# A transformer block with channel attention: the attention's norms read from PSUM, its PSUM copies on another engine, and a new order of the work

## The chip, the cores and the metric

The kernel runs on one core of a Trainium2 chip. The core has five engines with instruction queues of their own: TensorE (PE, matrix products; its weight loads are shown apart as PEld), VectorE (DVE), ScalarE (ACT), GpSimd (POOL) and SyncE (SP, which here only starts transfers). Each engine works through its queue in the order in which the program was written. The metric is the device time in microseconds from the first to the last instruction; the median of several executions counts.

## The reference, cut to what matters

The input is 16 images of 128 channels and 96 x 96 pixels in float32. Two residual steps follow each other:

```
xn1  = layernorm over channels(x)
q, k, v = xn1 @ wq.T, xn1 @ wk.T, xn1 @ wv.T        # 8 heads of 16 channels, over 9216 pixels
q, k = q / |q|, k / |k|                             # norms over the pixels, one for each channel
attn = softmax((q k^T) / 4)                         # 16 x 16 for each head
x    = x + (attn v) @ wp.T

xn2  = layernorm over channels(x)
h    = w_in xn2                                     # 1x1, to 512 channels
h    = depthwise 3x3 (h), then gelu
x    = x + w_out h                                  # 1x1, back to 128 channels
```

Since the attention works over channels and not over pixels, everything it needs of an image is the Gram matrix G = z z^T (128 x 128) of the normalized pixels z and their sum s. With the layer norm's scale folded into the weights and its shift b in bias terms c = W b, the inner product of two projected channels is w_i G w_j + (w_i s) c_j + c_i (w_j s) + N c_i c_j, with N = 9216 pixels. The squared norm of channel i is the same with i = j: w_i G w_i + 2 c_i (w_i s) + N c_i c_i.

## The kernel before, in words

**Tiling.** An image is cut into 8 bands of 12 rows (`BR`), a band into 3 units of 4 rows (`UR`, 384 pixels). Channels lie on the 128 partitions. The 512 hidden channels are four chunks of 128.

**Stages for an image.** `norm(i, False)` transposes pixels (`forth`, L572), takes the statistics (`stats`, L579, VectorE), computes the reciprocal deviation on GpSimd (L586, L590), scales on ScalarE (`scaled`, L617), adds the pixels into the Gram bank `g` in PSUM (`gram`, L631) and transposes back (`back`, L662; `place`, L668). `attention(s, i)` (L700 to L820) turns G and s into a 128 x 128 matrix `mwT` and a column `d`. `norm(i, True)` applies them (`mix`, L530; `mixed`, L539), adds x, and normalizes again (L572, L579, L621, L662, L666). Then `conv_job` makes one chunk of one band: 1x1 products on TensorE (`hidden`, L845), their copies from PSUM to SBUF on ScalarE (`kept`, L850), the nine taps of the depthwise filter partly as products on ScalarE (L861) that are added by accumulating transfers (L869), partly on VectorE (`tap`, L865, 128 x 1152 elements each), then gelu on ScalarE (L873). In some bands the fourth chunk is computed on TensorE instead (`by_matmuls`, L916, gelu L922). `ffn_out` makes the output product (L939) and adds it to x on VectorE (L946).

**Attention before.** It is a chain of 16 steps, each on one engine, in one PSUM bank. VectorE copies G and s from PSUM (`gs`, L728). TensorE transposes s to a row (L733), which VectorE copies (`srow`, L737). TensorE computes u = G W (L742), adds the one-partition bias term s c to it (L743), and makes the row s W (L745). VectorE copies u (L752), makes the row sW + N c (L753), and then the elementwise products u * W (L755) and (sW + N c) * c (L756), all 256 columns wide for q and k together and kept in a large tile `wide` that is taken from the pool of x tiles. TensorE sums both down the partitions for the norms (L763, L764) and makes k q^T from u and the rows (L769, L770). VectorE bounds the norms (L774), GpSimd takes the power -1/2 (L778), VectorE scales (L782, L784), TensorE transposes (L788), ScalarE takes the exponential (L793), VectorE masks, sums and divides (L798 to L801), TensorE makes the product with the output projection (L805), VectorE copies it (`y`, L809), TensorE makes the last two products (L813, L814) and VectorE copies them out (`mwT`, `d`, L818, L819).

**What sets the order.** Every piece of work is handed to a planner (`Plan.op`) with its engine, an assumed duration in ns, the tokens it reads and writes, and a due place. The due place is a number of conv jobs plus an offset for the kind of work from the table `AT`; at the same engine the smaller one goes first. `Plan.order` plays the program with the assumed durations, buffers and queues, and the work is then written out in the order of the starts that came out. This is done while the program is built; on the chip each engine keeps that order and waits where it must. So a change to an assumed duration, to a token or to the table moves instructions anywhere in the program. Image 0's attention uses one of four PSUM banks `h` that the other products share; the later images' use the Gram bank `g` itself, of which there is only one. `wide` stands on one of the two tiles of the x pool (`x1`).

Of the kernel before, what the change touches and what calls it, by code (L numbers as in the profile page):

```python
# [9 lines left out]
F32 = mybir.dt.float32  # L10
AF = mybir.ActivationFunctionType
ALU = mybir.AluOpType
# [6 lines left out]
BR = 12  # L19
# [10 lines left out]
X1_BUFS, XB_BUFS, PR_BUFS, H3_BUFS, ZT_BUFS = 2, 6, 5, 10, 3  # L30
IN_TURN = ("tr", "h3", "pr", "xb", "x1")
AT = dict(
    weights=5.95, zeros=1.3, load_a=-24.9, forth_a=-15.4, stats_a=-14.45, variance_a=-16.5, power_a=0.1,
    scaled_a=-8.2, gram=-10.45, back_a=-24.05, place_a=-20.25, attention=-20, mix=-9.75, residual=-0.2,
    mixed=-5.2, add_x=13.3, forth_b=-13.25, stats_b=-9.65, variance_b=-14, power_b=-10.85, shift_b=-26,
    scaled_b=4.45, back_b=-25.35, place_b=4.85, halo=7.55, hidden=0.1, kept=-2.95, product=-12.5,
    products=4.8, add_last=-15, tap=3.1, add_first=31.85, gelu=-8.35, conv=-0.05, conv_gelu=-13.5,
    out=4.05, add=-3.25, store=7.05,
)
STEP = dict(scaled=0.3, hidden=0.1, products=0.5, tap=0.166, conv=1.6, conv_tap=0.03, out=0.8, out_part=0.05)  # L40
SLACK = 300
# [164 lines left out]
def tile_restormer_block(  # L206
# [24 lines left out]
    nc = tc.nc  # L231
    B, C, H, W = x.shape
    P = 128
# [6 lines left out]
    NTOK = H * W  # L240
# [20 lines left out]
    ident = const.tile([P, P], F32, name="ident")  # L261
# [3 lines left out]
    ones = const.tile([P, 1], F32, name="ones")  # L265
# [15 lines left out]
    nc.scalar.dma_start(out=dw, in_=w_dw.rearrange("(n p) o kh kw -> p n (o kh kw)", p=P))  # L281

    wvb = const.tile([P, 1], F32, name="wvb")
    none = const.tile([P, 1], F32, name="none")
    wqkT = const.tile([P, 2 * P], F32, name="wqkT")
    cqk = const.tile([1, 2 * P], F32, name="cqk")
# [10 lines left out]
    keep = ctx.enter_context(tc.tile_pool(name="keep", bufs=2))  # L297
# [37 lines left out]
    grams, mats, h3s, staged = {}, {}, {}, {}  # L335
# [3 lines left out]
    op = plan.op  # L339
# [59 lines left out]
    def weights(p):  # L399

        mine = [("h3", ("weights", k)) for k in range(2)]
        v, names = staged, iter(range(99))
# [36 lines left out]
        def centred():  # L439
            pc = v["pc2"] = bank(("weights", "centred"))  # L440
            nc.tensor.matmul(pc[:, : 2 * P], lhsT=v["centre"], rhs=wqkT, start=True, stop=True)
            nc.tensor.matmul(pc[:, 2 * P : 3 * P], lhsT=v["wvT"], rhs=v["w1centre"], start=True, stop=True)
            nc.tensor.matmul(pc[:, 3 * P : 3 * P + 1], lhsT=v["wvT"], rhs=b1, start=True, stop=True)

        def keep_centred():
            nc.vector.tensor_copy(wqkT, v["pc2"][:, : 2 * P])
            nc.vector.tensor_copy(wv_sb, v["pc2"][:, 2 * P : 3 * P])
            nc.vector.tensor_copy(wvb, v["pc2"][:, 3 * P : 3 * P + 1])

        def biases():  # L450
            v["pc"] = bank(("weights", "biases"))[:1, : 2 * P]
# [23 lines left out]
        pc = ("h", ("weights", "centred"))  # L475
# [224 lines left out]
    def attention(s, i):  # L700


        places_of = dict(srow="ma", kq="ma", em="ma", y="ma", gs="mb", e="mb", a="mb")
        columns = dict(ps_s=128, ps_u=256, ps_r=0, ps_n=128, ps_kq=256, ps_qk=384, ps_y=0, ps_m=128, ps_d=256)
        v = {}
        apart = i == 0
        mine = [("h", ("attention", i)) if apart else ("g", i), ("m", i)]

        def sb(shape, tag, pool=att):
            v[tag] = pool.tile(shape, F32, tag=places_of.get(tag, tag), name=f"{tag}_{i}")  # L710
            return v[tag]

        def ps(shape, tag):

            c = columns[tag]
            v[tag] = (bank(("attention", i)) if apart else grams[i])[: shape[0], c : c + shape[1]]
            return v[tag]

        def step(engine, ns, also=()):
            def add(f):  # L720
                op(engine, ns, s, f, [("w", "qk")], [*mine, *also], ns + 200 + SLACK)
            return add

        wide = [("x1", ("attention", i))]

        @step("DVE", 210, [("g", i)])
        def _():
            nc.vector.tensor_copy(sb([P, P + 1], "gs"), grams[i][:, : P + 1])  # L728
            v["gsb"], v["s"] = v["gs"][:, :P], v["gs"][:, P:]

        @step("PE", 220)
        def _():
            nc.tensor.matmul(ps([1, P], "ps_s"), lhsT=v["s"], rhs=ident, start=True, stop=True)  # L733

        @step("DVE", 200)
        def _():
            nc.vector.tensor_copy(sb([1, P], "srow"), v["ps_s"])  # L737

        @step("PE", 1290)
        def _():  # L740

            nc.tensor.matmul(ps([P, 2 * P], "ps_u"), lhsT=v["gsb"], rhs=wqkT, start=True, stop=False)  # L742
            nc.tensor.matmul(v["ps_u"], lhsT=v["srow"], rhs=cqk, start=False, stop=True)  # L743

            nc.tensor.matmul(ps([1, 2 * P], "ps_r"), lhsT=v["s"], rhs=wqkT, start=True, stop=True)  # L745

        @step("DVE", 1400, wide)
        def _():
            t = x1pool.tile([P, BR * W], F32, tag="x", name=f"wide_{i}")
            for k, (rows_, tag) in enumerate([(P, "u"), (1, "srqk"), (P, "prod"), (1, "prow")]):  # L750
                v[tag] = t[:rows_, 2 * P * k : 2 * P * (k + 1)]
            nc.vector.tensor_copy(v["u"], v["ps_u"])  # L752
            nc.vector.scalar_tensor_tensor(v["srqk"], cqk, float(NTOK), v["ps_r"], ALU.mult, ALU.add)  # L753

            nc.vector.tensor_mul(v["prod"], v["u"], wqkT)  # L755
            nc.vector.tensor_mul(v["prow"], v["srqk"], cqk)  # L756

        @step("PE", 1320, wide)
        def _():
            pn = ps([P, 2], "ps_n")  # L760
# [11 lines left out]
        @step("DVE", 80)  # L772
# [12 lines left out]

        @step("PE", 110)
        def _():
            nc.tensor.transpose(ps([P, P], "ps_qk"), v["kq"], ident)  # L788

        @step("ACT", 2900)  # L790
        def _():

            nc.scalar.activation(sb([P, P], "e"), v["ps_qk"], AF.Exp, scale=v["rq"])  # L793

        @step("DVE", 700)
        def _():
# [10 lines left out]
        @step("DVE", 200)  # L807
        def _():
            nc.vector.tensor_copy(sb([P, P], "y"), v["ps_y"])  # L809

        @step("PE", 300)
        def _():
            nc.tensor.matmul(ps([P, P], "ps_m"), lhsT=wv_sb, rhs=v["y"], start=True, stop=True)  # L813
            nc.tensor.matmul(ps([P, 1], "ps_d"), lhsT=v["y"], rhs=wvb, start=True, stop=True)  # L814

        @step("DVE", 290)
        def _():
            nc.vector.tensor_copy(sb([P, P], "mwT", keep), v["ps_m"])  # L818
            nc.vector.tensor_copy(sb([P, 1], "d", keep), v["ps_d"])  # L819
            mats[i] = v["mwT"], v["d"]  # L820

    def h3_of(g, n):
# [201 lines left out]
```

## Time and profile before

| | before |
|---|---|
| time, median of 3 | 4276.48 us (4270.45 to 4277.21) |
| profiled span | 4280.8 us |
| VectorE taps, L865 | 3554.6 us busy in 2592 instructions |
| ScalarE products, L861 | 1907.7 us busy in 1422 instructions (1307.9 and 599.8) |
| TensorE conv, output and hidden products, L916, L939, L845 | 1305.4, 1158.5 and 1043.3 us busy |
| first tap starts | 98.64 us |
| attention of image 1, first to last copy | 224.57 to 251.30 us |

The page gives busy time of each engine, the span in 40 slices, the chain of work that ended last, and the costliest groups of instructions. In a group's line stand the source line, the engine, the operation, the output and inputs by name, shapes, count, and behind the bar the busy time, the mean duration and the idle time of the engine ahead of the group with what ended it. Durations of neighbours on one engine overlap a little, so that the sum of durations is larger than the time they hold the engine. A line of the timeline has the start, the length, engine, line, operation and, in brackets, idle time and what ended it. A line of the waits has the waiting engine and line, the one waited for, the total, the number and the longest.

### The profile page before, as it was taken

To read this page: it belongs to the slowest core of one execution; us is meant where nothing else is said; L and a number is where in the kernel's file an instruction comes from. 1 tells how busy PE (TensorE), PEld (TensorE's weight loads), DVE (VectorE), ACT (ScalarE), POOL (GpSimd) and SP (SyncE) were. 2 spreads that over 40 slices of the span, in tenths; PEclk is the share of its full clock that TensorE was granted. 3 is DMA by queue.
4 is the path that set the end of the run, shared out by engine and by line. 5 is a ranking of instruction groups with operands and counts; after the bars stand their busy time and mean duration, and the time that the engine had idled before them with its cause. 6 is when DMAs were issued, how large, how long until landed. Compare 5 with 4: busy or idle time off the path is not lost.

```text
span 4280.8 us, 52546 instructions
## 1 busy us (share of the span) xinstructions
PE 4201.1 (98%) x17453; PEld 2677.0 (63%) x17453; DVE 4141.5 (97%) x4766; ACT 4074.4 (95%) x7278; POOL 2423.4 (57%) x2331
## 2 busy tenths in 40 slices
PE   8999999999999999999999999999999999999999
PEld 6566666666666666666666665666656666666555
DVE  6999999999999999999999999999999999999999
ACT  4999999999999999999999999999999999999996
POOL 4556556555556556656565665556656555555432
PEclk9999999999999999999999999999999999999999
DMA  2889899998998989989898998989889898998997
GB/s 86 181 181 202 184 200 196 191 199 187 194 195 191 193 186 209 194 186 204 178 194 185 192 200 179 198 186 202 184 181 201 187 198 190 191 194 168 187 187 162
DMA packets 197887, 802.87 MB, mean 188 GB/s; under 512 B 22896, under 2 KB 24304, under 8 KB 197616
## 3 DMA queue, kind: packets, MB, share of 16 engines
q0 software_dynamic: 158112, 647.70, 78.3%
q1 hardware_dynamic: 37152, 151.01, 9.7%
q8 instruction: 138, 2.26, 0.2%
q10 hardware_dynamic: 2352, 0.81, 0.1%
q14 instruction: 133, 1.09, 0.1%
HBM read 148.26 MB, written 75.50 MB: 52 GB/s over the span
## 4 chain that ended last, share of the span: by engine, by line
PE 55%; ACT 21%; DVE 14%; DMA 5%; issue 3%; POOL 2%; ACTq 0%; POOLq 0%; DVEq 0%
PE h L916 16%; PE h L939 13%; DVE h L865 12%; PE h L845 11%; ACT pr L861 5%; DMA h<-pr 3%; PE g L631 3%; PE h L530 3%; ACT h L850 3%; ACT h L861 2%; ACT zT L621 2%; ACT h L873 2%; PE pB_a L662 2%; PE pB_b L662 2%; ACT zT L617 2%
## 5 line engine op out<-in xcount | busy, mean ns | idle before, releaser
L865 DVE SCALAR_TENSOR_TENSOR h<-h,dw,h 128x1152 f32<-128x1152 f32 x2592 | 3554.6, 1409 | 17.3 <-ACT h L861 14.0
L861 ACT ACTIVATE pr<-h,dw 128x1152 f32<-128x1152 f32 x976 | 1307.9, 1357 | 9.7 <-DMA pr<-pr 9.4
L916 PE MATMUL h<-xn,comp 128*128 128x384 f32 x3564 | 1305.4, 487 | 5.0 <-ACT h L850 3.1
L939 PE MATMUL h<-h,woutT 128*128 128x384 f32 x3072 | 1158.5, 489 | 7.3 <-ACT h L850 3.4
L845 PE MATMUL h<-xn,winT 128*128 128x384 f32 (+1 forms) x2676 | 1043.3, 501 | 5.4 <-ACT h L850 2.7
L916 PEld LDWEIGHTS h<-xn,comp 128*128 128x128 f32 x3564 | 652.4, 190 | 420.6 <-ACT h L850 13.5
L869 POOL DMA_DIRECT2D pr<-pr x531 | 498.8, 939 | 680.8 <-ACT pr L861 478.2
L939 PEld LDWEIGHTS h<-h,woutT 128*128 128x128 f32 x3072 | 560.1, 190 | 356.6 <-issue 15.0
L850 ACT COPY h<-h 128x384 f32<-128x384 f32 (+1 forms) x1338 | 702.0, 590 | 34.1 <-PE h L845 25.0
L869 POOL DMA_DIRECT2D h<-pr x445 | 437.9, 993 | 503.5 <-DVE h L865 117.3
L845 PEld LDWEIGHTS h<-xn,winT 128*128 128x128 f32 x2676 | 484.4, 190 | 323.7 <-issue 53.1
L861 ACT ACTIVATE h<-h,dw 128x1152 f32<-128x1152 f32 x446 | 599.8, 1347 | 5.1 <-PE h L939 3.2
L873 ACT ACTIVATE h<-h 128x1152 f32<-128x1152 f32 x448 | 556.6, 1243 | 42.2 <-DMA h<-pr 39.9
L590 POOL TENSOR_TENSOR rstd_a<-ve_a,mhalf 128x4 f32<-128x4 f32 x288 | 520.0, 1806 | 11.4 <-POOL ve_a L586 0.2
L590 POOL TENSOR_TENSOR rstd_b<-ve_b,mhalf 128x4 f32<-128x4 f32 x288 | 492.8, 1715 | 10.3
L621 ACT ACTIVATE zT<-pT_b,nb_b,rstd_b 128x128 f32<-128x128 f32 x1132 | 452.4, 559 | 6.4 <-DVE nb_b L594 6.4
L586 POOL TENSOR_SCALAR ve_b<-st_b 128x4 f32<-128x4 f32 x288 | 286.4, 994 | 260.0 <-DVE st_b L579 254.2
L586 POOL TENSOR_SCALAR ve_a<-st_a 128x4 f32<-128x4 f32 x288 | 292.6, 1016 | 227.1 <-DVE st_a L579 223.0
L617 ACT ACTIVATE zT<-pT_a,rstd_a 128x128 f32<-128x128 f32 x1080 | 330.3, 461 | 23.6 <-POOL rstd_a L590 23.3
L631 PE MATMUL g<-zT 128*128 128x129 f32 x2304 | 307.4, 276 | 0.0
L530 PE MATMUL h<-xn,mwT 128*128 128x384 f32 x768 | 293.7, 490 | 5.8 <-ACT h L850 4.8
L631 PEld LDWEIGHTS g<-zT 128*128 128x128 f32 x2304 | 282.9, 193 | 1.5 <-ACT zT L617 0.5
(156 smaller groups left out, 3698.3 us busy)
## 6 DMA issues: line engine op xcount, KB each, us to landing
pr<-pr POOLq DMA_DIRECT2D x531, 576.0 KB, 6.2
h<-pr POOLq DMA_DIRECT2D x445, 576.0 KB, 6.9
x<-in_x_dram SPq DMA_DIRECT2D x128, 576.0 KB, 6.1
out_dram<-x SPq DMA_DIRECT2D x127, 576.0 KB, 4.7
x<-in_x_dram POOLq DMA_DIRECT2D x122, 576.0 KB, 7.2
out_dram<-x SPq DMA_DIRECT2D x3, 192.0 KB, 1.9
weights<-in_L_conv_w_in_dram ACTq DMA_DIRECT2D x1, 256.0 KB, 10.9
weights<-in_L_conv_w_out_dram ACTq DMA_DIRECT2D x1, 256.0 KB, 11.7
```

The source lines that it names most:

```text
L586: nc.gpsimd.tensor_scalar(ve, d["mv"][:, :, 2], 1.0 / C, EPS, ALU.mult, ALU.add)
L590: nc.gpsimd.tensor_tensor(rstd, d["ve"], mhalf, ALU.pow)
L621: nc.scalar.activation(zT(q)[:, k, :P], d["pT", q][:, k, :], AF.Identity, bias=d["nb"][:, t : t + 1], scale=d["rstd"][:, t : t + 1],)
L631: nc.tensor.matmul(grams[i][:, : P + 1], lhsT=zt[:, :P], rhs=zt, start=(q == 0 and k == 0), stop=(q == NU * TPU // QT - 1 and k == QT - 1),)
L845: nc.tensor.matmul(rows(ph), lhsT=winT[:, n, :], rhs=window(xn, r0 + r, e - r, 1), start=True, stop=True)
L850: nc.scalar.copy(window(h1_, r, e - r, 1), rows(d.pop(("ph", r))))
L861: nc.scalar.activation(to, shifted(t), AF.Copy, scale=dw[:, n, t : t + 1])
L865: nc.vector.scalar_tensor_tensor(h3, shifted(t), dw[:, n, t : t + 1], h3, ALU.mult, ALU.add)
L869: nc.gpsimd.dma_start(out=to, in_=d["pr", t], accum_op=ALU.add)
L873: nc.scalar.activation(h3, h3, AF.Gelu)
L916: nc.tensor.matmul(d["pc"], lhsT=comp[:, t, :], rhs=window(xn, r0 + dy, UR, dx), start=(t == 0), stop=(t == 8),)
L939: nc.tensor.matmul(rows(d["po"]), lhsT=woutT[:, n, :], rhs=h3s[g, n][:, s * UR : (s + 1) * UR, :], start=(k == 0), stop=(k == NCH - 1),)
```

## The change

The norms and the product k q^T no longer need the bias in u. The norms take the form above: TensorE sums u * W down the partitions and multiplies the sum s with W into a column (`ps_c`), and four small operations on VectorE combine the two with columns that are made once from the weights (`ccol`: 2c and N c c). k q^T is made from u, s and c by three products instead of two. So the transpose of s, its row copy, the bias term of u and the wide row products go, and so does the copy of q's half of u: the product u * W reads PSUM itself. The copies that remain (`gs`, k's halves of u and of the row, `y`, `mwT`, `d`) are made by ScalarE. The chain has 14 steps. `wide` now has two parts with a token each, so that VectorE's and ScalarE's writes to it are not ordered by the planner. All offsets in `AT` have new values. The rest of the kernel is as before. The diff, cut to its core:

```diff
 AT = dict(
-    weights=5.95, zeros=1.3, load_a=-24.9, forth_a=-15.4, stats_a=-14.45, variance_a=-16.5, power_a=0.1,
-    scaled_a=-8.2, gram=-10.45, back_a=-24.05, place_a=-20.25, attention=-20, mix=-9.75, residual=-0.2,
-    mixed=-5.2, add_x=13.3, forth_b=-13.25, stats_b=-9.65, variance_b=-14, power_b=-10.85, shift_b=-26,
-    scaled_b=4.45, back_b=-25.35, place_b=4.85, halo=7.55, hidden=0.1, kept=-2.95, product=-12.5,
-    products=4.8, add_last=-15, tap=3.1, add_first=31.85, gelu=-8.35, conv=-0.05, conv_gelu=-13.5,
-    out=4.05, add=-3.25, store=7.05,
+    weights=8.1, zeros=0.25, load_a=-21.3, forth_a=-15.05, stats_a=-18, variance_a=-18.05, power_a=-1.8,
+    scaled_a=0.55, gram=-6.85, back_a=-25.85, place_a=-18.35, attention=-17.8, mix=-10.5, residual=4.7,
+    mixed=-4.65, add_x=14, forth_b=-14.75, stats_b=-10.65, variance_b=-15.9, power_b=-13.85,
+    shift_b=-25.75, scaled_b=3.95, back_b=-24.6, place_b=5.05, halo=9.05, hidden=0.85, kept=-0.9,
+    product=-13.2, products=5.45, add_last=-13.7, tap=3.45, add_first=27.05, gelu=-5.15, conv=0.55,
+    conv_gelu=-14.15, out=4.35, add=-4.2, store=7.05,
 )
...
+            for z in range(2):
+                to = pc[:, 3 * P + 1 + z : 3 * P + 2 + z]
+                nc.tensor.matmul(to, lhsT=v["wqkT"][:, z * P : (z + 1) * P], rhs=b1, start=True, stop=True)
...
+            c = v["pc2"][:, 3 * P + 1 : 3 * P + 3]
+            nc.vector.tensor_scalar(ccol[:, 0, :], c, 2.0, None, ALU.mult)
+            nc.vector.scalar_tensor_tensor(ccol[:, 1, :], c, NTOK / 2.0, ccol[:, 0, :], ALU.mult, ALU.mult)
+            nc.vector.tensor_scalar(ncq, cqk[:, :P], float(NTOK), None, ALU.mult)
...
-        @step("DVE", 210, [("g", i)])
+        @step("ACT", 200, [("g", i)])
-            nc.vector.tensor_copy(sb([P, P + 1], "gs"), grams[i][:, : P + 1])
+            nc.scalar.copy(sb([P, P + 1], "gs"), grams[i][:, : P + 1])
...
-            nc.tensor.matmul(ps([1, P], "ps_s"), lhsT=v["s"], rhs=ident, start=True, stop=True)
-            nc.vector.tensor_copy(sb([1, P], "srow"), v["ps_s"])
-            nc.tensor.matmul(ps([P, 2 * P], "ps_u"), lhsT=v["gsb"], rhs=wqkT, start=True, stop=False)
-            nc.tensor.matmul(v["ps_u"], lhsT=v["srow"], rhs=cqk, start=False, stop=True)
-            nc.tensor.matmul(ps([1, 2 * P], "ps_r"), lhsT=v["s"], rhs=wqkT, start=True, stop=True)
+            nc.tensor.matmul(ps([P, 2 * P], "ps_u"), lhsT=v["gsb"], rhs=wqkT, start=True, stop=True)
+            nc.tensor.matmul(ps([1, P], "ps_r"), lhsT=v["s"], rhs=wqkT[:, :P], start=True, stop=True)
+            v["ps_k"] = ps([1, 2 * P], "ps_r")[:, P:]
+            nc.tensor.matmul(v["ps_k"], lhsT=v["s"], rhs=wqkT[:, P:], start=True, stop=True)
...
-            nc.vector.tensor_copy(v["u"], v["ps_u"])
-            nc.vector.scalar_tensor_tensor(v["srqk"], cqk, float(NTOK), v["ps_r"], ALU.mult, ALU.add)
-            nc.vector.tensor_mul(v["prod"], v["u"], wqkT)
-            nc.vector.tensor_mul(v["prow"], v["srqk"], cqk)
+        @step("DVE", 210, wide, mine, [])
+            nc.vector.tensor_add(v["sqn"], v["ps_r"][:, :P], ncq)
+        @step("ACT", 300, wide[1:], mine, [])
+            nc.scalar.copy(v["uk"], v["ps_u"][:, P:])
+            nc.scalar.copy(v["sk"], v["ps_k"])
+        @step("DVE", 350, wide[:1], mine, [])
+            nc.vector.tensor_mul(v["prod"], v["ps_u"], wqkT)
...
-                nc.tensor.matmul(pn[:, z : z + 1], lhsT=v["prod"][:, zs], rhs=ones, start=True, stop=False)
-                nc.tensor.matmul(
-                    pn[:, z : z + 1], lhsT=v["prow"][:, zs], rhs=ones[0:1, :], start=False, stop=True
-                )
+                nc.tensor.matmul(pc[:, z : z + 1], lhsT=wqkT[:, zs], rhs=v["s"], start=True, stop=True)
+                nc.tensor.matmul(pn[:, z : z + 1], lhsT=v["prod"][:, zs], rhs=ones, start=True, stop=True)
...
-            nc.tensor.matmul(kq, lhsT=v["u"][:, P:], rhs=wqkT[:, :P], start=True, stop=False)
-            nc.tensor.matmul(kq, lhsT=v["srqk"][:, P:], rhs=cqk[:, :P], start=False, stop=True)
+            nc.tensor.matmul(kq, lhsT=v["uk"], rhs=wqkT[:, :P], start=True, stop=False)
+            nc.tensor.matmul(kq, lhsT=v["sk"], rhs=cqk[:, :P], start=False, stop=False)
+            nc.tensor.matmul(kq, lhsT=cqk[:, P:], rhs=v["sqn"], start=False, stop=True)
...
-            nc.vector.tensor_scalar(sb([P, 2], "n2"), v["ps_n"], 1e-24, None, ALU.max)
+            nc.vector.tensor_mul(n2, v["ps_c"], ccol[:, 0, :])
+            nc.vector.tensor_add(n2, n2, ccol[:, 1, :])
+            nc.vector.tensor_add(n2, v["ps_n"], n2)
+            nc.vector.tensor_scalar(n2, n2, 1e-24, None, ALU.max)
...
-        @step("DVE", 200)
-            nc.vector.tensor_copy(sb([P, P], "y"), v["ps_y"])
+        @step("ACT", 160)
+            nc.scalar.copy(sb([P, P], "y"), v["ps_y"])
...
-        @step("DVE", 290)
-            nc.vector.tensor_copy(sb([P, P], "mwT", keep), v["ps_m"])
-            nc.vector.tensor_copy(sb([P, 1], "d", keep), v["ps_d"])
+        @step("ACT", 250)
+            nc.scalar.copy(sb([P, P], "mwT", keep), v["ps_m"])
+            nc.scalar.copy(sb([P, 1], "d", keep), v["ps_d"])
```

More of the change, by code (lines that the diff above doesn't have):

```diff
@@ L283, in tile_restormer_block @@
     wvb = const.tile([P, 1], F32, name="wvb")
+    ccol = const.tile([P, 2, 2], F32, name="ccol")
+    ncq = const.tile([1, P], F32, name="ncq")
     none = const.tile([P, 1], F32, name="none")
@@ L700, in attention @@
     def attention(s, i):
-        places_of = dict(srow="ma", kq="ma", em="ma", y="ma", gs="mb", e="mb", a="mb")
-        columns = dict(ps_s=128, ps_u=256, ps_r=0, ps_n=128, ps_kq=256, ps_qk=384, ps_y=0, ps_m=128, ps_d=256)
+        places_of = dict(kq="ma", em="ma", y="ma", gs="mb", e="mb", a="mb")
+        columns = dict(ps_u=0, ps_r=256, ps_c=256, ps_n=384, ps_kq=0, ps_qk=128, ps_y=256, ps_m=0, ps_d=384)
         v = {}
@@ L717, in ps, with step @@
             return v[tag]
-        def step(engine, ns, also=()):
+        def step(engine, ns, also=(), reads=(), writes=mine):
             def add(f):
-                op(engine, ns, s, f, [("w", "qk")], [*mine, *also], ns + 200 + SLACK)
+                op(engine, ns, s, f, [("w", "qk"), *reads], [*writes, *also], ns + 200 + SLACK)
             return add
-        wide = [("x1", ("attention", i))]
-        @step("DVE", 210, [("g", i)])
+        wide = [("x1", ("attention", i), k) for k in range(2)]
@@ L727, in _ @@
+        @step("ACT", 200, [("g", i)])
         def _():
-            nc.vector.tensor_copy(sb([P, P + 1], "gs"), grams[i][:, : P + 1])
+            nc.scalar.copy(sb([P, P + 1], "gs"), grams[i][:, : P + 1])
             v["gsb"], v["s"] = v["gs"][:, :P], v["gs"][:, P:]
-        @step("PE", 220)
+        @step("PE", 760)
         def _():
-            nc.tensor.matmul(ps([1, P], "ps_s"), lhsT=v["s"], rhs=ident, start=True, stop=True)
-        @step("DVE", 200)
-        def _():
-            nc.vector.tensor_copy(sb([1, P], "srow"), v["ps_s"])
@@ L739, in _ @@
-        @step("PE", 1290)
+            nc.tensor.matmul(ps([P, 2 * P], "ps_u"), lhsT=v["gsb"], rhs=wqkT, start=True, stop=True)
[3 more added lines that the diff above has]
+        @step("DVE", 210, wide, mine, [])
+        def _():
+            t = v["wide"] = x1pool.tile([P, BR * W], F32, tag="x", name=f"wide_{i}")
+            v["prod"], v["uk"], v["sk"], v["sqn"] = (
+                t[:, : 2 * P], t[:, 2 * P : 3 * P], t[:1, 3 * P : 4 * P], t[:1, 4 * P : 5 * P]
+            )
+            nc.vector.tensor_add(v["sqn"], v["ps_r"][:, :P], ncq)
@@ L740, in _ @@
+        @step("ACT", 300, wide[1:], mine, [])
         def _():
[L742 to L747, printed above, removed]
+            nc.scalar.copy(v["uk"], v["ps_u"][:, P:])
+            nc.scalar.copy(v["sk"], v["ps_k"])
+        @step("DVE", 350, wide[:1], mine, [])
@@ L748, in _ @@
         def _():
[L749 to L756, printed above, removed]
@@ L758, in _ @@
-        @step("PE", 1320, wide)
+            nc.vector.tensor_mul(v["prod"], v["ps_u"], wqkT)
+        @step("PE", 1100, wide)
         def _():
-            pn = ps([P, 2], "ps_n")
+            pn, pc = ps([P, 2], "ps_n"), ps([P, 2], "ps_c")
             for z in range(2):
                 zs = slice(z * P, (z + 1) * P)
-                nc.tensor.matmul(pn[:, z : z + 1], lhsT=v["prod"][:, zs], rhs=ones, start=True, stop=False)
-                nc.tensor.matmul(
-                    pn[:, z : z + 1], lhsT=v["prow"][:, zs], rhs=ones[0:1, :], start=False, stop=True
-                )
+                nc.tensor.matmul(pc[:, z : z + 1], lhsT=wqkT[:, zs], rhs=v["s"], start=True, stop=True)
+                nc.tensor.matmul(pn[:, z : z + 1], lhsT=v["prod"][:, zs], rhs=ones, start=True, stop=True)
@@ L768, in _ @@
             kq = ps([P, P], "ps_kq")
-            nc.tensor.matmul(kq, lhsT=v["u"][:, P:], rhs=wqkT[:, :P], start=True, stop=False)
-            nc.tensor.matmul(kq, lhsT=v["srqk"][:, P:], rhs=cqk[:, :P], start=False, stop=True)
-        @step("DVE", 80)
+            nc.tensor.matmul(kq, lhsT=v["uk"], rhs=wqkT[:, :P], start=True, stop=False)
+            nc.tensor.matmul(kq, lhsT=v["sk"], rhs=cqk[:, :P], start=False, stop=False)
+            nc.tensor.matmul(kq, lhsT=cqk[:, P:], rhs=v["sqn"], start=False, stop=True)
@@ L773, in _ @@
+        @step("DVE", 320)
         def _():
-            nc.vector.tensor_scalar(sb([P, 2], "n2"), v["ps_n"], 1e-24, None, ALU.max)
+            n2 = sb([P, 2], "n2")
+            nc.vector.tensor_mul(n2, v["ps_c"], ccol[:, 0, :])
+            nc.vector.tensor_add(n2, n2, ccol[:, 1, :])
+            nc.vector.tensor_add(n2, v["ps_n"], n2)
+            nc.vector.tensor_scalar(n2, n2, 1e-24, None, ALU.max)
         @step("POOL", 700)
@@ L805, in _ @@
             nc.tensor.matmul(ps([P, P], "ps_y"), lhsT=v["a"], rhs=wpT, start=True, stop=True)
-        @step("DVE", 200)
+        @step("ACT", 160)
         def _():
-            nc.vector.tensor_copy(sb([P, P], "y"), v["ps_y"])
+            nc.scalar.copy(sb([P, P], "y"), v["ps_y"])
         @step("PE", 300)
```

## The prediction

> **What bounds the kernel now.** I read the page first (busy shares, then the chain that ended last), then the stretches of 250 us, then the waits of TensorE, then one attention in the timeline.
>
> ```profile
> PE 4201.1 (98%) x17453; PEld 2677.0 (63%) x17453; DVE 4141.5 (97%) x4766; ACT 4074.4 (95%) x7278; POOL 2423.4 (57%) x2331
> ...
> PE 55%; ACT 21%; DVE 14%; DMA 5%; issue 3%; POOL 2%; ACTq 0%; POOLq 0%; DVEq 0%
> ```
>
> Three engines are nearly full, and the chain runs mostly over TensorE. The stretches (columns: PE, PEld, DVE, ACT, POOL busy) show the same without the two ends:
>
> ```profile
> 600.00:850.00 250.00, 249.21 (x1045) 159.58 (x1044) 247.44 (x282) 246.39 (x449) 149.37 (x139) 1.00 0.92 195
> ...
> 2600.00:2850.00 250.00, 244.47 (x1021) 154.90 (x1020) 242.92 (x270) 240.06 (x435) 147.11 (x136) 1.00 0.90 190
> 3350.00:3600.00 250.00, 247.20 (x1034) 158.17 (x1033) 244.96 (x280) 243.20 (x439) 142.80 (x138) 1.00 0.91 192
> ```
>
> TensorE idles about 3 us in 250, VectorE 5, ScalarE 7. TensorE's "busy" is mostly real: in the tail, 18 matmul passes of 384 columns take 5.81 us, 0.323 us each, and the conv line's 3564 passes at that pace are 1151 us of its 1305 busy[...]. So I take TensorE as the bound, with ScalarE next to it, since what TensorE waits for is nearly always ScalarE's emptying of PSUM:
>
> ```profile
> PE pT_a L572 <- ACT zT L617: 11.3, 17, 2.9
> PE pB_a L662 <- ACT zT L617: 8.1, 6, 2.6
> ...
> PE h L939 <- ACT h L850: 3.4, 4, 2.2
> PE h L916 <- ACT h L850: 3.1, 8, 0.7
> ```
>
> One attention (image 1) runs from 224.57, its first copy, to 251.30, its last, under the convolution of image 0. Its front half:
>
> ```profile
> 229.07 0.60 PE L742 MATMUL g<-wqkT,gs 128*128 128x256 f32 x2
> ...
> 229.60 0.69 PE L743 MATMUL g<-cqk,srow 1*128 1x256 f32 x2
> ...
> 230.22 0.59 PE L745 MATMUL g<-wqkT,gs 128*1 128x256 f32 x2
> ...
> 230.85 0.42 DVE L752 COPY wide<-g 128x256 f32<-128x256 f32 x1 [0.57 <-PE g L745]
> ...
> 231.20 0.40 DVE L753 SCALAR_TENSOR_TENSOR wide<-cqk,g 1x256 f32<-1x256 f32 x1
> ...
> 231.52 0.41 DVE L755 TENSOR_TENSOR wide<-wide,wqkT 128x256 f32<-128x256 f32 x1
> ...
> 231.86 0.41 DVE L756 TENSOR_TENSOR wide<-wide,cqk 1x256 f32<-1x256 f32 x1
> ```
>
> A row of one partition costs DVE as much as 128. Sixteen images in about 4180 us are 261 each, so after the first tap at 98.64 image 1's is due near 360, some 100 us behind this chain's end: apart from image 0 it is work, not latency, that counts.
>
> [...]
>
> **TensorE, per image.** Out: the transpose of the sum (0.38, L733), the bias term of u (0.62 from its start to the next), and the 256-column row product (0.52 by its neighbours' starts). In: two 128-column row products, which I put at 0.38 and 0.26 by L733. Balance -0.88. In the second cluster the two bias sums of the norms (0.31 a pair of passes) become two products with the sum vector at the same 0.31; one more one-partition term enters kq, 0.41 as L770's. Balance -0.47 an image, up to -0.77 with the issue gaps ahead of L733: -7.5 to -12 us over 16. I take -8. The new order switches between matmuls and transposes 1002 times against 980[...].
>
> **VectorE, per image,** by durations: out are gs 0.29, srow 0.27, u 0.42, the bias products 0.41, y 0.28, mwT 0.28, d 0.15; the 256-wide row sum shrinks to 128 (-0.12). The product now reads PSUM at the same 0.41. The norm's one small operation becomes four dependent ones, +3 x 0.155. Balance -1.76, or -28 us in all. Start to start, neighbours overlap (128-wide 0.20, 256-wide 0.34, with the small dependent ones at 0.20), which gives -1.1 and -17. Range -17 to -28.
>
> **ScalarE, per image,** takes gs, uk, sk, y, mwT and d. [...] So +13 to +24; I take 18. It eats a sixth of ScalarE's 7 us of idle in 250 and does not fill it.
>
> **Waits.** Two handovers go (PE-DVE-PE for the sum's row). New is VectorE's small sum, then ScalarE's two copies, then VectorE's product, by turns on one bank. In the changed order exactly one tap (1.4 us) lies between VectorE's two ends in each attention after the first, sometimes with a small operation more[...]. If ScalarE is late, the product stalls with taps queued behind it; if VectorE is late, ScalarE stalls with PSUM copies behind it, for which TensorE waits. Bounds: 0 (hidden under the tap) to 1.4 us an image. The nearest wait in the old trace, n on L770, cost 8.0 us over 11 of 16 images; I take 0.5 an image, on VectorE, which the 1.1 to 1.76 saved covers.
>
> **Start.** The first tap starts at 98.64. Image 0's attention chain (52.12 to 70.95) is on the way to it, and image 1's next load is issued at 60.61, when the chain frees its buffer; losing two handovers gives some 1.5 us there. The changed order also holds back image 1's statistics until after the first residual adds (two groups ahead of the first tap instead of four), worth 2 or 3 us more on the way to the first tap. That work is only moved, so I count 2 to 3 in all. The three constants added to the weights are three small VectorE operations, about 0.5 us, under PE's transposes. The tail has the same order of matmuls and taps in its last 20 us: nothing.
>
> **Sum.** TensorE -8, switches +1 to +4 (I take +2), start -2.5, and ScalarE's extra against VectorE's relief by their shares of the chain: 0.21 x 18 - 0.14 x 22 = +0.7. That is -8. The retimed table moves everything else too: convolution passes now stand in closer runs (34 changes from conv straight to output product, before 375), so a conv bank is held for a shorter time and is copied sooner. I give that -4, an estimate of a fifteenth of the 63 us that TensorE idles after the first 100. Forecast 4276.5 - 12 = 4264.
>
> **Rivals.**
> - The reordering also closes TensorE's gaps. For it: 63 us of idle, waits spread over many lines, shorter bank holds, less VectorE work to block on. Against it: the waits are on ScalarE, which gets more work. A third recovered is 21: 4264 - 21 = 4243.
> - A wash: the saved 8 us are lost in the new turns and in ScalarE's copies, since TensorE waits for ScalarE anyway. Time 4276.
> - Slower: ScalarE becomes the bound. For it: all the waits above, and six more copies standing ahead of evictions; +18 on the path and little of TensorE's saving kept: 4276 + 18 = 4294. Against it: ScalarE's 7 us of idle per 250.
>
> **Numbers.** Forecast 0.42, closed gaps 0.20, wash 0.15, slower 0.23. Faster by over 0.2% (below 4268): 0.36 of the forecast's share and all of the closed gaps, 0.56. Same: 0.06 of the forecast and 0.13 of the wash, 0.19. Slower by over 0.2%: 0.25. The range leaves out about a tenth on each side: 4235, beyond the closed gaps, to 4296, with ScalarE's +18 and a little of the 22 us that stalls of a whole tap would cost.
>
> **What would show it.** Right: PE busy down by about 8 us, DVE by 17 to 28, ACT up by 13 to 24; the product's wait on ScalarE short; the first tap before 97; ScalarE waits of TensorE about as before. Wrong: TensorE's waits on ScalarE copies grow by over 15 us (slower), DVE waits for the uk copies reach a tap each, or the idle of TensorE in the stretches falls below 2 in 250 (much faster). A reordering that shifts stretches far from any attention would make the prediction wrong whatever the attention does.

## The result and the profile after

The changed kernel takes 4244.81 us (median of 6 runs, 4241.34 to 4253.49) against 4276.84 (4270.45 to 4278.85) for the kernel before, run beside it: a ratio of 0.9933 with an interval of 0.9920 to 0.9946. That is faster by 29 us by the ratio and by 32 by the medians, inside the range of the prediction and some 20 us below its likeliest time. Ratios of other kernels below are also to the kernel before, run on the same chip as each; a ratio step of 0.001 is 4.3 us. The expected times below suppose 4276 us for the kernel before, whose median was 4267 to 4275 on the chips of the later runs, so I compare by ratios.

The profiled span fell from 4280.8 to 4242.3. That is more than the medians show, because the profiled execution of the kernel before took 4282.52 us, 6 above its median. From the page after, busy times and the shares of the chain that ended last:

```profile
PE 4175.6 (98%) x17457; PEld 2667.1 (63%) x17457; DVE 4121.0 (97%) x4705; ACT 4080.1 (96%) x7374; POOL 2403.9 (57%) x2331
...
PE 49%; ACT 20%; DVE 13%; DMA 5%; issue 3%; POOL 1%; POOLq 0%; ACTq 0%; DVEq 0%
```

TensorE's busy time fell by 25.5 us, nearly three times what its attention lost, and its idle (span less busy) from 79.7 to 66.7. The 38.5 us of span are made up of these two. I break the busy part down further below. The stretches after (columns: PE, PEld, DVE, ACT, POOL busy, TensorE's clock, DMA share, GB/s):

```profile
600.00:850.00 250.00, 249.08 (x1068) 160.94 (x1068) 247.53 (x286) 248.93 (x461) 146.50 (x145) 1.00 0.94 197
2600.00:2850.00 250.00, 247.31 (x1052) 159.24 (x1051) 247.51 (x278) 247.64 (x455) 149.40 (x141) 1.00 0.95 199
```

Neither busy time nor the count of products measures progress here. In the first stretch TensorE is busy 249 us in both kernels; 1068 of its products fall into it, 1045 before, but products differ in size. The taps, 162 to an image, are all alike. The same stretch for the taps alone, L865 before and then L876 after (columns: the stretch, VectorE busy, TensorE's clock, DMA share, GB/s):

```profile
600.00:850.00 250.00, 214.78 (x157) 1.00 0.92 195
```

```profile
600.00:850.00 250.00, 214.67 (x157) 1.00 0.94 197
```

There are 157 taps in both, so the changed kernel gains nothing in this stretch. In the second one it has 157 and the kernel before 155.

TensorE's waits after:

```profile
PE h L950 <- ACT h L861: 7.2, 12, 2.0
...
PE pB_b L671 <- ACT xn L677: 4.5, 5, 1.9
...
PE pT_a L581 <- ACT zT L630: 2.8, 8, 0.6
...
PE pT_a L581 <- ACT zT L626: 2.1, 3, 1.1
...
PE pB_a L671 <- ACT zT L626: 1.4, 1, 1.4
```

The two largest waits of before, on the scaling of the first norm (`zT`, L617 then, L626 now; 11.3 and 8.1), are down to 2.1 and 1.4. Adding up every line of this view, TensorE waits 58.7 us in all, before 73.7; for any `zT` of ScalarE 8.0, before 25.0; for the conv jobs' copies `h` 17.6, before 18.1. So the waits that went are those of the first norm (21.9 before, 3.9 after), and not of the attention.

The attention itself, image 1, in the timeline after (start, length, engine, line):

```profile
245.82 0.38 PE L746 MATMUL g<-wqkT,gs 128*1 128x128 f32 x2
...
246.29 0.28 DVE L754 TENSOR_TENSOR wide<-g,ncq 1x128 f32<-1x128 f32 x1
...
246.56 1.36 ACT L872 ACTIVATE pr<-h,dw 128x1152 f32<-128x1152 f32 x1
...
247.72 0.58 ACT L933 ACTIVATE h<-h 128x384 f32<-128x384 f32 x1
...
248.09 0.37 ACT L758 COPY wide<-g 128x128 f32<-128x128 f32 x1
248.23 0.25 ACT L759 COPY wide<-g 1x128 f32<-1x128 f32 x1
...
248.89 0.41 DVE L763 TENSOR_TENSOR wide<-g,wqkT 128x256 f32<-128x256 f32 x1
```

VectorE, ScalarE and VectorE take their turns on the bank. ScalarE comes 1.5 us after VectorE's small sum, because a product (L872) and a gelu (L933) stand ahead of it in its queue; the last step follows 0.4 us after ScalarE's end.

### The profile page after: what moved, and what is told of

Read it like the earlier page. It is cut to its first block, busy times and chain, and to the rows that moved or that the text cites. A ratio compares the mean times of both kernels' runs of the same rounds, so it can differ in the third digit from the quotient of the medians.

```text
span 4242.3 us, 52552 instructions
## 1 busy us (share of the span) xinstructions
PE 4175.6 (98%) x17457; PEld 2667.1 (63%) x17457; DVE 4121.0 (97%) x4705; ACT 4080.1 (96%) x7374; POOL 2403.9 (57%) x2331
## 4 chain that ended last, share of the span: by engine, by line
PE 49%; ACT 20%; DVE 13%; DMA 5%; issue 3%; POOL 1%; POOLq 0%; ACTq 0%; DVEq 0%
PE h L927 15%; PE h L950 11%; DVE h L876 11%; PE h L856 10%; ACT pr L872 5%; DMA h<-pr 3%; PE g L640 3%; PE h L539 3%; ACT h L861 3%; ACT h L884 2%; ACT h L872 2%; ACT zT L630 2%; PE pB_a L671 2%; PE pT_b L581 1%; PE pB_b L671 1%
## 5 line engine op out<-in xcount | busy, mean ns | idle before, releaser
L876 DVE SCALAR_TENSOR_TENSOR h<-h,dw,h 128x1152 f32<-128x1152 f32 x2592 | 3563.1, 1410 | 12.6 <-ACT h L872 9.3
L872 ACT ACTIVATE pr<-h,dw 128x1152 f32<-128x1152 f32 x976 | 1319.9, 1376 | 8.9 <-DMA pr<-pr 8.8
L927 PE MATMUL h<-xn,comp 128*128 128x384 f32 x3564 | 1268.1, 486 | 4.3 <-ACT h L861 2.6
L950 PE MATMUL h<-h,woutT 128*128 128x384 f32 x3072 | 1120.9, 488 | 12.2 <-ACT h L861 7.2
L856 PE MATMUL h<-xn,winT 128*128 128x384 f32 (+1 forms) x2676 | 1055.2, 501 | 10.7 <-ACT h L861 3.7
L861 ACT COPY h<-h 128x384 f32<-128x384 f32 (+1 forms) x1338 | 722.2, 605 | 21.2 <-PE h L856 18.7
L880 POOL DMA_DIRECT2D h<-pr x445 | 425.2, 963 | 520.6 <-DVE h L876 183.2
L872 ACT ACTIVATE h<-h,dw 128x1152 f32<-128x1152 f32 x446 | 603.8, 1361 | 1.8 <-PE h L950 0.2
L599 POOL TENSOR_TENSOR rstd_a<-ve_a,mhalf 128x4 f32<-128x4 f32 x288 | 492.8, 1712 | 10.5 <-POOL ve_a L595 0.2
L595 POOL TENSOR_SCALAR ve_b<-st_b 128x4 f32<-128x4 f32 x288 | 297.3, 1041 | 257.0 <-DVE st_b L588 253.9
L595 POOL TENSOR_SCALAR ve_a<-st_a 128x4 f32<-128x4 f32 x288 | 275.8, 958 | 265.7 <-DVE st_a L588 263.6
L626 ACT ACTIVATE zT<-pT_a,rstd_a 128x128 f32<-128x128 f32 x1080 | 339.3, 492 | 13.6 <-POOL rstd_a L599 13.4
L539 PE MATMUL h<-xn,mwT 128*128 128x384 f32 x768 | 284.0, 489 | 2.1 <-ACT zT L630 0.7
## 6 DMA issues: line engine op xcount, KB each, us to landing
weights<-in_L_conv_w_in_dram ACTq DMA_DIRECT2D x1, 256.0 KB, 11.3
```

Source lines behind the costliest of these rows:

```text
L595: nc.gpsimd.tensor_scalar(ve, d["mv"][:, :, 2], 1.0 / C, EPS, ALU.mult, ALU.add)
L599: nc.gpsimd.tensor_tensor(rstd, d["ve"], mhalf, ALU.pow)
L856: nc.tensor.matmul(rows(ph), lhsT=winT[:, n, :], rhs=window(xn, r0 + r, e - r, 1), start=True, stop=True)
L861: nc.scalar.copy(window(h1_, r, e - r, 1), rows(d.pop(("ph", r))))
L872: nc.scalar.activation(to, shifted(t), AF.Copy, scale=dw[:, n, t : t + 1])
L876: nc.vector.scalar_tensor_tensor(h3, shifted(t), dw[:, n, t : t + 1], h3, ALU.mult, ALU.add)
```

## The experiments

**1. One half at a time.** First the new attention with the old table of offsets, planned anew, and the old attention with the new table.

```diff
 AT = dict(
-    weights=8.1, zeros=0.25, load_a=-21.3, forth_a=-15.05, stats_a=-18, variance_a=-18.05, power_a=-1.8,
+    weights=5.95, zeros=1.3, load_a=-24.9, forth_a=-15.4, stats_a=-14.45, variance_a=-16.5, power_a=0.1,
...
```

> The changed attention, planned with the old table of offsets. Work theory (the attention's removed instructions bring the gain): near the changed kernel, 4245 to 4252. Order theory (the new table brings about 24 of the 32 us, the attention about 8): 4262 to 4270, with the runs of convolution passes interleaved with output products as before.

> The old attention, planned with the new table. Work theory: near the kernel before, 4268 to 4277. Order theory: 4250 to 4256. If the table only pays together with the attention for which it was found, both this and the kernel with the new attention and the old table stay above 4265.

Measured: 1.0002 (0.9993 to 1.0012) and 1.0005 (0.9998 to 1.0013). Neither half alone gives anything beyond the 0.001 that these intervals resolve. So the gain is not a sum of an attention's part and an order's part; with the orders that came out here, each needs the other. Each of the two is a single planned order, and none beside it was run, so a bad draw of an order is not excluded. With the old table TensorE still waits 22.7 us for `zT`, as before. The old attention with the new table has the close runs of conv passes (41 changes straight from a conv to an output product, against 375 before and 34 after), and gains nothing: close runs alone do not bring the gain.

**2. The old order held fixed.** The planner sees the old steps with their old durations and tokens, so the order of all other instructions is exactly that of before; only the bodies of the attention's steps are exchanged.

```diff
-            nc.vector.tensor_copy(sb([P, P + 1], "gs"), grams[i][:, : P + 1])
+            nc.scalar.copy(sb([P, P + 1], "gs"), grams[i][:, : P + 1])
...
-            nc.tensor.matmul(ps([1, P], "ps_s"), lhsT=v["s"], rhs=ident, start=True, stop=True)
+            pass
...
```

> The old program order kept exactly for every other instruction, with the new attention's instructions put in the old steps' places (the planner still counts the old durations). Work theory: 4276 minus 8 to 30, at the work's share. Forecast by the prediction's sum for the attention alone: TensorE 8 to 9 us less, VectorE about 28 less, ScalarE about 28 more, 4266 to 4272. A rival in which ScalarE's copies cost what they add: 4277 to 4295.

The same with the six copies left on VectorE (`nc.vector.tensor_copy` in place of `nc.scalar.copy`):

> The old order, the new attention's instructions in the old steps' places, with all PSUM copies on VectorE. If ScalarE's six copies ate the 9 us that TensorE saves in that order: 4262 to 4269 where before has 4276. If the old order takes no gain from the attention's work at all: 4272 to 4280.

Measured: 1.0009 (0.9999 to 1.0019) with the copies on ScalarE, 0.9978 (0.9969 to 0.9987) with them on VectorE. The new instructions without the move to ScalarE are worth 0.0022, 9.4 us (5.5 to 13), about what TensorE's attention lost. Moving the copies to ScalarE in this order costs 0.0031, or 13 us, loose by some 6: the whole of that gain. The pages show both engines' load as intended; with the copies on ScalarE and then on VectorE:

```profile
PE 4187.8 (98%) x17457; PEld 2667.6 (62%) x17457; DVE 4122.6 (97%) x4705; ACT 4083.4 (96%) x7374; POOL 2394.9 (56%) x2331
```

```profile
PE 4185.6 (98%) x17457; PEld 2670.4 (63%) x17457; DVE 4137.6 (97%) x4801; ACT 4075.1 (96%) x7278; POOL 2403.0 (56%) x2331
```

TensorE's waits in the old order with the copies on ScalarE:

```profile
PE pT_a L581 <- ACT zT L626: 7.6, 14, 2.3
PE h L539 <- ACT h L863: 6.9, 5, 1.9
PE pB_a L671 <- ACT zT L626: 5.4, 4, 2.6
```

The waits for the first norm's scaling stay (21.9 us for the `zT` of both norms), and the mix (L539) waits 6.9 us for conv copies, before 4.8.

**3. The new order held fixed, with the copies on VectorE.** The planner's calls stay as in the changed kernel; the six bodies change.

```diff
-            nc.scalar.copy(sb([P, P + 1], "gs"), grams[i][:, : P + 1])
+            nc.vector.tensor_copy(sb([P, P + 1], "gs"), grams[i][:, : P + 1])
...
```

> The changed program in exactly its order, with the six PSUM copies of each attention written for VectorE instead of ScalarE. VectorE theory (VectorE's queue, not TensorE's, sets the pace of an image): 17 to 25 us of VectorE come back, 4260 to 4270. ScalarE theory (TensorE waits for ScalarE's copies, so less there is gain): 4235 to 4243. TensorE theory: within 5 us of 4245.

Measured: 0.9932 (0.9917 to 0.9947), the same as the changed kernel. In the new order no difference shows between the engines that make the copies, to within 8 us. With the arithmetic fixed, the new order is worth 0.9978 to 0.9932, 20 us, with copies on VectorE, and 1.0009 to 0.9933, 32 us, with copies on ScalarE, each loose by some 7 us.

**4. Is it one lucky order?** The planner's slack of 300 ns a hand-over was set to 302, and, apart from that, 200 ns were added to each hand-over of the attention, which lengthens the chain in the plan. No instruction changes. (The chain has 16 steps after the change as before it, not 14: two steps go, and one is split into three. So the plan's chain grows by 3.2 us.)

```diff
-SLACK = 300
+SLACK = 302
```

> The changed kernel with the planner's allowance for latency at 302 instead of 300 ns, which changes nothing of the work and reshuffles the order a little. If the order is a lucky one that the table was picked for, this is 4252 to 4265; if the table gives good orders in general, within 6 us of 4245.

```diff
-                op(engine, ns, s, f, [("w", "qk"), *reads], [*writes, *also], ns + 200 + SLACK)
+                op(engine, ns, s, f, [("w", "qk"), *reads], [*writes, *also], ns + 200 + SLACK + 200)
```

> The changed kernel, planned as if each of the attention's 14 steps took 200 ns longer to hand over (2.8 us an image, the old chain's length), with no instruction changed. If the new table's order only pays when the planner may count on a short attention chain: within 8 us of the kernel before. If it is the work that counts and the order is good either way: within 6 us of the changed kernel, 4238 to 4251 where the kernel before has 4276.

Measured: 0.9937 (0.9919 to 0.9954) and 0.9934 (0.9919 to 0.9949). Three orders of this kind give the same time. The gain of the new attention with the new table doesn't hang on one order, nor on the attention's planned length.

**5. What a microsecond costs on each engine.** To the changed kernel, extra work is added in each attention, with the order kept: three more u products on TensorE, four 128 x 256 products on VectorE, or four copies of that size on ScalarE.

```diff
+            for _ in range(3):
+                nc.tensor.matmul(ps([P, 2 * P], "ps_u"), lhsT=v["gsb"], rhs=wqkT, start=True, stop=True)
             nc.tensor.matmul(ps([P, 2 * P], "ps_u"), lhsT=v["gsb"], rhs=wqkT, start=True, stop=True)
```

> The changed kernel in its order, with three more copies of the product u = G W in each attention, into the same PSUM columns: 0.43 each at the pace of 256 columns, 1.3 us an image, 21 in all. TensorE theory: paid in full, 4263 to 4268. VectorE theory: 4246 to 4255[...].

```diff
             nc.vector.tensor_mul(v["prod"], v["ps_u"], wqkT)
+            for _ in range(4):
+                nc.vector.tensor_mul(scr, wqkT, wqkT)
```

> The changed kernel in its order, with four more VectorE products of 256 columns in each attention, whose result nobody reads: about 0.34 to 0.41 each, 1.4 to 1.6 us an image, 22 to 26 in all. VectorE theory: paid in full, 4265 to 4271. TensorE theory: hidden but for a share of 0.14, 4247 to 4250.

```diff
             nc.scalar.copy(v["sk"], v["ps_k"])
+            for _ in range(4):
+                nc.scalar.copy(scr, wqkT)
```

> The changed kernel in its order, with four more ScalarE copies of 256 columns between SBUF tiles in each attention, whose result nobody reads: about 0.3 to 0.4 each, 1.2 to 1.6 us an image, 19 to 26 in all. If ScalarE sets the pace: 4262 to 4270. If VectorE or TensorE does: 4245 to 4253.

The added work, as groups of each trace (busy, mean ns):

```profile
L744 PE MATMUL g<-wqkT,gs 128*128 128x256 f32 x90 | 21.9, 379 | 0.0
```

```profile
L766 DVE TENSOR_TENSOR scr<-wqkT 128x256 f32<-128x256 f32 x64 | 27.0, 421 | 1.6
```

```profile
L762 ACT COPY scr<-wqkT 128x256 f32<-128x256 f32 x64 | 26.2, 410 | 1.5
```

In each image after the first the added products are six passes (L744); the kernel's own product, L745 here, is two more. Measured: TensorE 0.9980 (0.9974 to 0.9987), VectorE 0.9960 (0.9945 to 0.9975), ScalarE 0.9966 (0.9953 to 0.9979). Against 0.9933 that is 20 us for about 21 added on TensorE (48 products, 0.43 us each from start to start), 11.5 for about 26 on VectorE and 14 for 26 on ScalarE: slopes near 0.95, 0.45 and 0.55. (On the pages the busy times of the three engines rose by 18.8, 22.2 and 25.1.) Each slope is a difference of two ratios and loose, TensorE's by some 6 us, the other two by some 8. TensorE's is the highest, as it should be for the bound, but by these intervals its distance from ScalarE's is not settled. Each is also taken at one place in the attention only.

**6. Work taken away, and nothing else.** In the order of before, kept exactly, the bias terms of u and of the norms are left out; then the same in the order that the old attention gets from the new table.

```diff
-            nc.tensor.matmul(ps([1, P], "ps_s"), lhsT=v["s"], rhs=ident, start=True, stop=True)
+            pass
...
-            nc.tensor.matmul(v["ps_u"], lhsT=v["srow"], rhs=cqk, start=False, stop=True)
...
-            nc.vector.tensor_mul(v["prow"], v["srqk"], cqk)
...
```

> The kernel before in exactly its order, leaving out the transpose of the sum, its row copy, the bias term of u and the bias sums of the norms (1.6 us of TensorE and 0.7 of VectorE an image, 26 and 11 in all; the attention's bias terms are incomplete). TensorE theory: 26 at a slope near one and half of 11, so 4240 to 4250 where before has 4276. If the old order is held by something else (as the new attention in the old order, with no gain, suggests): 4265 to 4277.

> The old attention planned with the new table, in exactly that order, leaving out the same bias work as the kernel above (26 us of TensorE and 11 of VectorE in all). If the new table's order turns removed work into time and the old one does not: 4240 to 4252. If the slope is the same at both orders, the two kernels without bias work agree within 6 us.

Measured: 0.9946 (0.9929 to 0.9963), 23 us for 26 us of TensorE work; and 0.9975 (0.9965 to 0.9984), 13 us below its own base of 1.0005. About 11 us of VectorE's work went too, and at the slope above they would be worth 5, so TensorE's own part of the 23 is 18 to 23: in the old order its work is paid to a large part, as in the new one. In the order that doesn't fit, half of the work brings no time, though the difference of 10 us between the two is loose by 9. Where that half went, the traces don't show: TensorE's waits add up to 80.0 us there, only 2.2 more than with the whole attention, and the profiled execution of the latter, at 4288.30 us, is the slowest of its twenty (median 4276.85). Here are the largest waits of TensorE in that execution, for the whole old attention with the new table:

```profile
PE h L845 <- ACT h L850: 8.0, 7, 2.3
PE pB_a L662 <- ACT xn L666: 7.7, 4, 6.9
PE pB_a L662 <- ACT xn L668: 6.4, 6, 2.8
PE h L939 <- ACT h L850: 6.3, 7, 2.5
...
PE pT_a L572 <- ACT zT L617: 3.4, 7, 1.4
```

The waits for `zT` are as low as in the changed kernel (10.5 us in all). Others have come in their place: 25.9 us for the conv copies `h` (18.1 before) and 15.7 for `xn` (10.7), so that all waits together are 77.8, before 73.7.

## Why the prediction was right, and which of its terms was mis-sized

**TensorE is the bound: right,** as far as the slopes go. Added TensorE work costs 0.95 of itself, and removing 26 us of it, with 11 of VectorE's, gave 23.

**TensorE's attention, -8: right.** By groups, fifteen images, its eight lines before are 69.8 us busy and its eight lines after 61.0; for sixteen that is 9.4 less. The new instructions in the old order, with their copies on VectorE, measured 9.4. What the switches between matmuls and transposes cost was not measured, and the +2 for them was my estimate, with no run behind it: in the trace of before a group of three transposes (L662) lasts 0.33 us in the median from its start to the next line's, behind a matmul as behind other transposes.

**VectorE, -17 to -28: right;** the page has -20.5. **ScalarE, +13 to +24: over it by the durations, under it on the page.** The range was my estimate, and no trace shows it: that of before holds no copy of 128 columns on ScalarE, and its exponential of that size took 367 ns in the mean (L793). The six copies are 27.9 us by their groups, and 29 with image 0's, over the range; the first copy and k's took 368 and 392 ns.

```profile
L737 ACT COPY gs<-g 128x129 f32<-128x129 f32 x16 | 5.9, 368 | 0.0
L758 ACT COPY wide<-g 128x128 f32<-128x128 f32 x15 | 5.9, 392 | 0.3 <-DVE wide L754 0.3
L829 ACT COPY mwT<-g 128x128 f32<-128x128 f32 x15 | 4.5, 300 | 0.0
L759 ACT COPY wide<-g 1x128 f32<-1x128 f32 x15 | 4.1, 270 | 0.0
```

ScalarE's busy time rose by 5.7 only, and by 4.9 against the same order with the copies on VectorE (4075.2), while the 26 us added from SBUF in the fifth experiment raised it by 25.1. Overlap with neighbours may be the reason; no run separates that. Table loads have no part in the 5.7: ScalarE has 32 before and 32 after, none of them at a copy's line.

**The turns on one bank, 0.5 us an image (8 in all): a little high.** The product waited for ScalarE 4.9 us in all, in 7 images, and ScalarE for VectorE's sum 0.3; in image 1 its two copies took 0.39 us from the start of the first to the end of the second:

```profile
DVE wide L763 <- ACT wide L759: 4.9, 7, 1.0
```

**The start, -2.5: right for the first tap,** which starts at 95.4, before 98.64; image 0's attention takes 16.3 us from first to last copy, before 18.8. That the gain at the start reaches the end is not shown: with the longer plan of the fourth experiment the first tap starts at 99.27, and the ratio is the same 0.9934. **The tail: right,** 7.0 us in both from the end of the last tap (4273.8 before, 4235.3 after) to the end of the span.

**ScalarE's extra against VectorE's relief, +0.7: dependent on the order.** In the old order the move alone cost 13 us. In the new order it costs nothing, to within 8 us, which fits the term. Its weights were too low all the same: I had taken the shares of the chain that ended last (0.21 and 0.14), and the added work gives slopes of 0.55 and 0.45. In the sum the two errors cancel. So a share of one chain is not a price.

**The order, -4: this is the term that was mis-sized.** It was worth 20 us with the copies on VectorE and 32 with them on ScalarE. Its given reason, close conv runs, does not hold alone, by the first experiment. My argument against a larger gain, that TensorE's waits are on ScalarE and ScalarE gets more work, failed: the waits for `zT` fell from 25.0 to 8.0 us while ScalarE's work grew.

**Inside the range, but in part by luck.** The time is that of the rival to which I gave 0.20, the closed gaps, at 4243. The rival's way to it holds only in part: of the 63 us that TensorE idles after the first 100, it counted on 21, and 13 went. The sign that I had set for it (TensorE idle below 2 us in 250) did not come either: the three stretches idle 0.9, 2.7 and 2.8. And the forecast's own part for the attention, some -8, was +4 (0 to +8) where it could be measured with the order held, in the second experiment. So the range held because it was drawn wide enough to take in that rival, not because the forecast's sum was good. What I had written as a risk, that the new order shifts stretches far from any attention, is what the norms' waits point to.

Where did the 38.5 us of the profiled span go? TensorE's idle is 13.0 of it, all of it after the first 100 us, in which it idles 17 in both. Attention's products are 9.4. A further 10 or so are TensorE's clock, 0.996 of full speed in the mean before and 0.998 after: in the trace's record of the clock, 34.1 us before and 14.0 after are at half rate, so that 17 and 7 us are lost; half of the difference lies in the first 150 us. The remaining 6 lie inside the busy time, by subtraction; what they are is not shown.

This clock part belongs to the pair of executions, for the clock varies from one to the next: among 39 of the kernel before on one chip, the time is some 4 us longer for each 0.001 of clock that is missing. In the mean, the clock was 0.9962 to 0.9966 for the kernel before, 0.9972 for the changed kernel, and 0.9978 to 0.9985 for the three other kernels of the new attention in orders of the new table without added work, which makes 3 to 9 us, as an estimate. It is not the whole cause either: the new attention with the old table had 0.9975 and gained nothing.

A tap and the one 162 taps later are 261.2 us apart before and 259.4 after in the median. But the gain is not even. The changed kernel is ahead by 3.3 us at the first tap of image 0, by 4.0 at that of image 7, and by 38.5 at the last tap. This may belong to the one trace of before: the new attention with the old table, which gains nothing, is 13.6 us behind it at tap 1215 and 9.3 ahead at tap 2511.

How does the clock go with the waits? Two windows of 10 us of the kernel before (the column of 0.83 is the clock):

```profile
2064.00:2074.00 10.00, 10.00 (x38) 6.37 (x38) 8.92 (x14) 7.85 (x13) 6.52 (x6) 0.83 0.67 184
2190.00:2200.00 10.00, 8.40 (x30) 5.33 (x31) 6.92 (x9) 8.79 (x16) 6.33 (x8) 0.83 1.01 189
```

In the timeline of before, a wait for `zT` stands ahead of the half-rate part of the second of these, which begins at 2192.90:

```profile
2191.60 0.66 PE L572 MATMUL pT_a<-ident,x 128*128 128x128 f32 x4 [2.73 <-ACT zT L617]
...
2193.06 4.36 PE L939 MATMUL h<-h,woutT 128*128 128x384 f32 x8
```

Eight passes take 4.36 us where the tail's pace of 0.323 each gives 2.6. The trace's record of the clock has half rate here for 3.41 us. In the whole span of the kernel before its half-rate pieces are five of 3.41 us and, in the first 100 us, one of 6.83 and one of 10.24. The wait ahead of this one is 2.73 us. In the first of the two windows no such wait stands; the one-column products of an attention with a wait of 0.94 do. Over all fourteen traces, leaving out the first 160 us and the last 10, there are 21 such pieces: 18 have a wait of 2 to 7 us within 4 us of their start, and three have no wait over 0.94 but the one-column products of an attention. A wait is not always followed by one: the longest of the kernel before in that stretch, 2.95 us ending at 3006.72, was not. So I show what stands next to the half-rate pieces, and not what sets them off.

**What stays open.** With either attention the new table takes most of the waits for the norms' scaling away (25.0 us for `zT` before; 7.1 to 10.5 in the nine runs with the new table, 15.5 to 25.0 in the five with the old one). With the new attention all of TensorE's waits together fall too (56 to 61 us in the four kernels without added work, 73.7 before); with the old one waits for conv copies and `xn` take their place. So the loss of the `zT` waits alone is not what brings the time. Why the planner's order for the old attention has the others isn't settled: taking work away didn't remove them, so it is not the work alone. Another set of offsets for the old attention, or a neighbouring order of either mixed kernel, was not tried. Which of the table's offsets matters is not known.

## What to carry to other kernels

Work on the engine that sets the pace was paid nearly one to one here (0.95 by the added products), so price that first; work moved between engines that are nearly full has to be priced by adding some, not by their shares of one chain. A planned program's order is judged by holding it fixed and exchanging the instructions, and the other way round: each half alone showed nothing here, and together they gave 0.7%. A table of offsets was worth something only with the work that it came with. Read its effect from the sum of all waits and from the time of an image: one producer's waits fell without any gain here, and the number of products in a stretch rose where the kernel was no faster.

## What the runs showed of the hardware

A TensorE that is busy 98% of the time still lost time to its clock, about 17 us before and 7 after in the profiled pair; one wait of 2.73 us was followed by 3.4 us at half rate, another of 2.95 was not, and three half-rate pieces stand behind one-column products with no wait over 0.94 us. ScalarE's copies of 128 x 128 from PSUM took 286 to 392 ns in the mean (k's copy 392 in the new order and 331 in the old one), and a copy of one row 270; VectorE's of the same, in the new order with copies on VectorE, 272 to 283 and 269:

```profile
L820 DVE COPY y<-g 128x128 f32<-128x128 f32 x15 | 4.2, 283 | 0.0
...
L758 DVE COPY wide<-g 128x128 f32<-128x128 f32 x15 | 4.1, 272 | 0.0
L759 DVE COPY wide<-g 1x128 f32<-1x128 f32 x15 | 4.0, 269 | 0.0
```
